# Local attention with a 7x7 dilated convolution, then whitening: a row of the first image by single taps, interpolations cut in two, and a new order of sums

## The chip, the cores and the metric

The kernel runs on one core of a Trainium2 chip. The time is device microseconds of one execution, launch to end. The profile is a trace of one execution by the hardware profiler. Engines: PE is TensorE (PEld its weight loads), DVE is VectorE, ACT is ScalarE, POOL is GpSimd, SP is SyncE, whose queue issues most DMAs.

## What is computed

All data are 32-bit floats; x is 4 images of 256 channels and 64 x 64 pixels.

```python
# layer 0: attention weights from a 7x7 convolution with dilation 2, then local sums
k = conv(x, w1, padding=6, dilation=2) + b1      # 256 -> 128 channels
k = conv1x1(k, w2) + b2                          # 128 -> 49 channels
attn = softmax(k, axis=channels)                 # one weight per tap of a 7x7 window
xp = pad(x, 6)
shifts = stack([xp[:, :, 2*u:2*u+64, 2*v:2*v+64] for u in range(7) for v in range(7)])
y = einsum('bkchw,bkhw->bchw', shifts, attn)
# layer 1: whitening of y in 4 groups of 64 channels
# Sigma = covariance of a group over all images and pixels; 5 Newton steps towards Sigma^(-1/2)
out = whiten(y) * weight + bias
```

## The kernel before, in words

Both convolutions are folded into one, 256 channels to 49 taps. With dilation 2 an image falls into four planes by the parity of row and column, and on each plane the 7x7 convolution is undilated. It is computed in Winograd form over rows and columns with the points 1, -1, 2, -2, 1/2, 0 and infinity (`EVAL`).

**A row point** (`rows`, `prepare`, `conv_step`). For one row point of one image VectorE combines rows of x into a buffer `rb` (`row_eval`), then for each column point combines columns into `xh` (`col_eval`). TensorE multiplies `xh` by transformed weights `wr` (`conv_bank`, line 466) in three banks of column points, (1, -1, 0), (2, -2, infinity) and (1/2), each into one of two PSUM buffers `cv`; ScalarE evicts each bank into `pv` (L475). VectorE then interpolates over columns (`col_interp`, 22 operations of 162 columns) into `zz`. `prepare` of the next row point follows each bank in the program, so `xh` and `wr` are filled as TensorE frees them. When all row points are done, `row_interp` does the same 22 operations of 576 columns over rows, and one ScalarE activation of 2048 columns adds the bias (L535). The result is the image's logits. The helpers `add`, `sub` and `madd` (lines 265, 268, 272) issue every VectorE operation of these steps, so one line of the profile stands for many.

**Weights** of a row point are formed by VectorE once, in the first image that uses them, scaled by ScalarE, stored to DRAM (`gd`, L384) and loaded again for later images (L330). Row point 1/2 (number 5) is not a Winograd row in image 0: its combined weights `gb5` are kept in DRAM (`g5d`) and its transformed weights are formed in image 1 from that copy.

**Image 0** takes row points 1, -1, 2 and -2 (numbers 1 to 4) in Winograd form. Points 0, 1/2 and infinity go by `direct` (L554): for each of the seven column taps and two channel halves, matmuls of up to 512 columns add into one half of the PSUM tile `acc`; a row point has two halves, `sr` 0 and 1 (infinity has one). ScalarE copies half 0 into `zz` (L565) or one row of half 1 (L567), and VectorE adds the rest. Order on TensorE: infinity, row 1, 0 (half 0), row 2, 0 (half 1), row 3, 1/2 (both halves), row 4; then infinity of image 1 (`direct_inf`) and its row 0. In images 1 to 3 only infinity is direct.

**Softmax and sums.** For each image and column parity `softmax` transposes the logits (L680), takes the maximum (L688, L691), exponentials with their sums (L696), and normalises (L710). `move_terms` copies the weights of one plane `n` (16 in all) into `zt` (16 copies, L738) and SyncE stores them to `sd`; `load_band` loads them skewed, in two parts, into `band`, and VectorE transposes them in place (L766). `zt` and `band` have one buffer each. TensorE then multiplies transposed blocks of x (`make_block`, L780, evicted by L787) by the band (`weighted_sum`, L808). The sums of a plane are two halves, `first_half` and `second_half`, evicted by L822 into the slot of x; `turn_y` transposes y (L837, evicted by L844) and `moments` (L857) adds up the covariance. Three PSUM buffers `tp` serve every transpose.

**The order of the work.** TensorE's order is the program's own (`pe`). The other engines' orders come from the scheduler of the build, and each engine runs its list in that order. A hand-written plan cuts the convolutions of an image into eight parts of equal cost and calls, in the gap after each, softmax steps and halves of sums of the image before (`plan`, `gap`). Softmax of an image stands in gaps 1 and 2 of the next one; the eight halves of images 0 and 1 in gaps 3, 4 (two of them), 5, 6, 7, 8, 9 of the next image, where 8 and 9 are gaps 0 and 1 of the one after. Image 2's halves begin in gap 3, image 3's after all convolutions. x of later images is loaded by GpSimd's queue after the finished slot is spilled to DRAM (`move`), and y is loaded back for the end (`back`), where out is written (L1116 to L1135).

Of the kernel before, what the change touches and what calls it, by code (L numbers as in the profile page):

```python
# [31 lines left out]
def kernel(  # L32
# [230 lines left out]

    def add(o, a, b):
        return TT(o, a, b, ALU.add)  # L265

    def sub(o, a, b):
        return TT(o, a, b, ALU.subtract)

    def madd(o, a, f, b):  # L270

        return STT(o, a, f, b, ALU.mult, ALU.add)  # L272
# [4 lines left out]
    g5d = dram.tile([P, KS * NSK], F32, name="g5d")  # L277

    def row_weights(br):
# [8 lines left out]
        if br == 1:  # L288
            add(E, T[6], T[4])
            add(O, T[5], T[3])  # L290
            add(S0, E, O)
            add(E1, T[2], T[0])
            add(S1, E1, T[1])
        elif br == 2:
            sub(S0, E, O)
            sub(S1, E1, T[1])
        elif br == 3:
            madd(E, T[4], 4.0, T[6])
            madd(O, T[3], 4.0, T[5])
            madd(S0, O, 2.0, E)  # L300
            madd(E1, T[0], 4.0, T[2])
            madd(S1, T[1], 2.0, E1)
        elif br == 4:
            madd(S0, O, -2.0, E)
            madd(S1, T[1], -2.0, E1)
        else:
            madd(S0, T[6], 2.0, T[5])
            madd(S0, S0, 2.0, T[4])
            madd(S0, S0, 2.0, T[3])
            madd(S1, T[2], 4.0, T[0])  # L310
            madd(S1, T[1], 2.0, S1)
            add(S1, S1, S1)
            f = gb5.rearrange("p v a r k -> p (v a r k)")
            nc.scalar.mul(f, f, SCALE[5])
            nc.sync.dma_start(g5d, f)

    def weights(b, br, i):
# [17 lines left out]
        elif br == 5:  # L335

            f = rb[0].rearrange("p q r c w -> p (q r c w)")[:, : KS * NSK]
            if i == 0:
                nc.sync.dma_start(f, g5d)
# [40 lines left out]
        for bc in BANKS[i]:  # L380
            f = SCALE[bc] * (SCALE[br] if br != 5 else 1.0)
# [98 lines left out]
    def interpolate(pt, tmp, outs, cut):  # L480
# [9 lines left out]
        add(tmp, s1, s2)  # L490
        sub(s2, s1, s2)
        add(s1, s3, s4)
        sub(s4, s3, s4)
        add(s3, c0, c6)
        madd(hh, tmp, 10.0 / 9, hh)
        madd(hh, s1, -1.0 / 9, hh)
        madd(hh, s3, 2.5, hh)
        sub(s3, tmp, s3)
        madd(s1, tmp, -2.0, s1)
        madd(s1, c0, 1.5, s1)  # L500
        madd(s1, c6, -30.0, s1)
        madd(s3, s1, -1.0 / 6, s3)
        sub(tmp, s4, s2)
        madd(hh, s2, 16.0 / 9, hh)
        madd(hh, tmp, -1.0 / 9, hh)
        madd(tmp, hh, -3.0, tmp)
        sub(s2, s2, hh)
        madd(s2, tmp, -1.0 / 15, s2)
        madd(outs[0], lo(s1), 1.0 / 6, hi(c0))
        madd(outs[1], lo(tmp), 1.0 / 15, hi(s2))  # L510
        add(outs[2], lo(c6), hi(s3))
        nc.scalar.copy(outs[3], lo(hh))
# [5 lines left out]
    def col_interp(br, pv):  # L518
        pt = {b: pv[:K2, i] for i, b in enumerate(ORDER)}
        outs = phases(zz[:K2, br].rearrange("p q (w two) -> p q w two", two=2))  # L520
        cut = lambda t, k: t[:, :, 2 * k : 2 * (k + Q8)].rearrange("p q (b two) -> p q b two", two=2)
        interpolate(pt, it[:K2], outs, cut)

    def row_interp(b):
# [8 lines left out]
        interpolate(pt, ct.rearrange("p a b -> p (a b)")[:K2, : Q9 * W].rearrange("p (q w) -> p q w", w=W), outs, lambda t, k: t[:, k : k + Q8])  # L533
        f = lg[:K2].rearrange("p r w -> p (r w)")
        nc.scalar.activation(f, f, AF.Identity, bias=bias[:K2])  # L535
        logits[b] = lg
# [47 lines left out]
    rows = [(0, br) for br in (1, 2, 3, 4)]  # L584
# [16 lines left out]
    def conv_step(k, i):  # L601
# [3 lines left out]
        if k + 1 < len(rows):  # L605
            prepare(k + 1, i)
        if i == len(BANKS) - 1:
            col_interp(br, pvs.pop((b, br)))
            if k + 1 == len(rows) or rows[k + 1][0] != b:
                row_interp(b)  # L610

    def direct0(br, sr):
        if br == 5:
            direct(0, br, sr, acc[:, sr], [gb5[:, v, :, sr] for v in range(KS)], x5)
# [6 lines left out]
    for k in range(NR0):  # L623
        if k == 2:
            row_weights(5)
            x5 = store[4].rearrange("p c r w -> p (c r w)")[:, SH * W :].rearrange(
                "p (q r c w) -> p q r c w", q=Q8, r=2, c=NCC
            )
            row_eval(0, 5, [rb[0], rb[1], x5])
# [4 lines left out]
        elif k == 2:  # L634
            direct0(5, 0)
            direct0(5, 1)

            for sr in range(2):
                nc.scalar.copy(
                    gr0[:, :, :, sr].rearrange("p v a k -> p (v a) k"),  # L640
                    tap[:, UPOS[KS - 1 - 4 * sr]].rearrange("p v a k -> p (v a) k"),
                )
        if k == 1:
            for s in range(2, 4):
                load_x(s, s, nc.gpsimd)
    gpool.release()
# [27 lines left out]
    def softmax(b, pc, hf):  # L674

        lv = logits[b].rearrange("p r w -> p (r w)")
        lt = tp().rearrange("p (i h k) -> p i h k", i=NI, h=2)
        for i in range(NI):
            pe(
                nc.tensor.transpose(  # L680
                    lt[:, i].rearrange("p h k -> p (h k)")[:, :K2],
                    lv[:K2, bass.ds(2 * (NI * hf + i) * P + pc, P, 2)],
                    ident[:K2, :K2],
                )
            )
        nm = f"{b}_{pc}_{hf}"
        mx = work.tile([P, NI, 2], F32, tag="mx", name=f"mx_{nm}")
        nc.vector.tensor_reduce(mx, lt[:, :, :, :KT], AX.X, ALU.max)  # L688
        if hf == 0:
            terms[b, pc] = bpool.tile([P, 2, NCH, KT], F32, tag="d", name=f"d_{b}_{pc}", bufs=2)  # L690
        nc.vector.tensor_scalar(mx, mx, -1.0, None, ALU.mult)  # L691
        d = terms[b, pc][:, :, NI * hf : NI * (hf + 1)]
        s = work.tile([P, 2, NI], F32, tag="s", name=f"s_{nm}")
        for h in range(2):
            for i in range(NI):
                nc.scalar.activation(  # L696
                    d[:, h, i], lt[:, i, h, :KT], AF.Exp,
                    bias=mx[:, i, h : h + 1], accum_out=s[:, h, i : i + 1],
                )
        nc.vector.reciprocal(s, s)  # L700
        rm = work.tile([P, 2, NI, KS], F32, tag="rm", name=f"rm_{nm}")
        nc.vector.tensor_tensor(
            rm.rearrange("p h i v -> p (h i) v"),
            s.rearrange("p h i -> p (h i)").unsqueeze(2).to_broadcast([P, NCH, KS]),
            cmask.unsqueeze(1).to_broadcast([P, NCH, KS]),
            ALU.mult,
        )
        for h in range(2):
            dh = d[:, h].rearrange("p i (u v) -> p i u v", u=KS)
            nc.vector.tensor_tensor(  # L710
                dh, dh, rm[:, h].unsqueeze(2).to_broadcast([P, NI, KS, KS]), ALU.mult
# [35 lines left out]
    BAND = ((0, 3), (3, 8))  # L747
# [26 lines left out]
    def make_block(n, m):  # L774
# [18 lines left out]
        ((6, 21, 31), (4, 16, 23), (3, 16, 19), (7, 25, 32), (5, 17, 27)),  # L793
# [129 lines left out]
    def bands(n):  # L923
# [4 lines left out]
        if n - 1 in done:  # L928
            load_band(n, 1)
            move_terms(n + 1)  # L930

    def second_half(n):
        turn_y(n, 0)
        turn_y(n, 1)
        weighted_sum(n, 1, 0)
        turn_y(n, 2)
        weighted_sum(n, 1, 1)
        turn_y(n, 3)
        make_block(n, 5)
# [19 lines left out]
    def soft(b, pc):  # L959
        for hf in range(2):  # L960
            softmax(b, pc, hf)
# [3 lines left out]
    for b in range(B):  # L965
# [5 lines left out]
        if b + 2 < B:  # L971

            plan(b + 1, 3, hs[0])
            plan(b + 1, 4, *hs[1:3])
            plan(b + 1, 5, hs[3])
            plan(b + 1, 5, finish)
            for j in range(4):
                plan(b + 1, 6 + j, hs[4 + j])
# [3 lines left out]
    for b in range(B):  # L982
        for j in range(2):
            plan(b + 1, j if b == B - 1 else j + 1, lambda b=b, j=j: soft(b, j))
# [124 lines left out]
    n = 0  # L1109
# [60 lines left out]
```

## Time and profile before

| | us |
|---|---|
| median of 3 runs | 819.41 (816.88 to 820.16) |
| the profiled execution | 819.8 |
| its span, first to last instruction | 818.0 |
| TensorE busy | 719.5 |
| VectorE busy | 598.4 |
| ScalarE busy | 365.3 |
| mean granted clock of TensorE | 0.947 |

A page's timeline shows one line per group of equal instructions: its start, its length, engine, line and operation, the tiles written and read, and in brackets the idle time of the engine ahead of it with what ended that idle time. A table of windows gives busy time of each engine in a stretch of the span. Matmuls are pipelined, so a busy TensorE isn't TensorE at its peak. VectorE's operations overlap a little at their ends: an operation on 576 columns lasts 0.75 us, and the next starts 0.67 us after it.

### The profile page before, as it was taken

The numbers are of one execution on the slowest core, as the hardware profiler recorded it, in microseconds if no ns is written. First come the engines' busy times: TensorE is split into PE (matmuls) and PEld (weight loads), VectorE is DVE, ScalarE is ACT, GpSimd is POOL, SyncE is SP. The second block draws the span as 40 slices with busy tenths as digits, with TensorE's granted clock in tenths as the row PEclk, the third lists the DMA queues.
The fourth block names the chain that finished last, engine by engine and source line by source line (L and its number), as shares of the span: only waits on it lengthen the run. The fifth ranks groups of instructions, "written<-read, shape, count | busy, mean of one in ns | idle before, by whom it ended". The sixth has DMA issues, their size and how long they took to land.

```text
span 818.0 us, 18531 instructions
## 1 busy us (share of the span) xinstructions
PE 719.5 (88%) x7540; PEld 555.6 (68%) x7540; DVE 598.4 (73%) x1300; ACT 365.3 (45%) x1067; POOL 35.1 (4%) x45
## 2 busy tenths in 40 slices
PE   5789997975768999999879999989999487998997
PEld 1356672655746996789759968888898366886443
DVE  2799999599779767989797579898966732214443
ACT  1323332214565344267553333686434575553443
POOL 0320000300000010000100100000000100000000
PEclk9979998997979999999989999998999698999999
DMA  8993001320744275045934931155411554310577
GB/s 332 197 285 111 32 36 65 107 82 20 199 153 133 105 230 149 19 165 149 250 103 130 262 104 31 48 162 183 139 53 46 212 211 123 109 46 1 232 305 286
DMA packets 57837, 114.66 MB, mean 140 GB/s; under 512 B 21607, under 2 KB 40856, under 8 KB 56472
## 3 DMA queue, kind: packets, MB, share of 16 engines
q1 hardware_dynamic: 53624, 88.31, 34.2%
q0 software_dynamic: 4128, 25.17, 10.5%
q8 instruction: 59, 0.97, 0.5%
q14 instruction: 26, 0.21, 0.1%
HBM read 66.83 MB, written 46.63 MB: 139 GB/s over the span
## 4 chain that ended last, share of the span: by engine, by line
PE 31%; DVE 24%; DMA 10%; ACT 9%; issue 4%; SPq 0%; POOL 0%; DVEq 0%; ACTq 0%; POOLq 0%
PE y L808 10%; PE tp L1116 7%; PE cv L466 6%; ACT zt L738 4%; DMA slot<-in_x_dram 4%; DVE zz L272 4%; DMA sd<-zt 3%; PE sig L857 3%; PE tp L780 3%; DVE xh L272 3%; DVE pv L272 3%; PE tp L837 2%; DMA spill<-slot 2%; DVE rb L272 2%; DVE band L766 1%
## 5 line engine op out<-in xcount | busy, mean ns | idle before, releaser
L466 PE MATMUL cv<-xh,wr 128*49 128x128 f32 (+1 forms) x4576 | 263.0, 276 | 3.7 <-DVE xh L265 3.5
L466 PEld LDWEIGHTS cv<-xh,wr 128*49 128x49 f32 x4576 | 256.1, 124 | 9.8 <-issue 5.3
L808 PE MATMUL y<-band,xb 128*128 128x320 f32 (+2 forms) x640 | 163.0, 391 | 21.7 <-ACT xb L787 15.1
L808 PEld LDWEIGHTS y<-band,xb 128*128 128x128 f32 x640 | 112.4, 205 | 38.1 <-ACT xb L787 18.2
L766 DVE STREAM_TRANSPOSE band<-band 128x960 f32<-128x960 f32 (+1 forms) x32 | 48.2, 1508 | 59.5 <-DMA band<-sd 42.8
L738 ACT COPY zt<-d 32x112 f32<-32x112 f32 x224 | 62.9, 281 | 37.6 <-DMA sd<-zt 19.0
L837 PE MATMUL tp<-ident,slot 128*128 128x128 f32 x256 | 52.8, 303 | 16.4 <-ACT yt L844 12.1
L837 PEld LDWEIGHTS tp<-ident,slot 128*128 128x128 f32 x256 | 43.1, 203 | 31.6 <-ACT yt L844 14.6
L822 ACT ACTIVATE slot<-y,pivot 128x512 f32<-128x512 f32 x64 | 43.1, 732 | 41.9 <-PE y L808 41.8
L475 ACT COPY pv<-cv 113x486 f32<-113x486 f32 (+1 forms) x66 | 31.7, 480 | 66.1 <-PE cv L466 66.0
L844 ACT COPY yt<-tp 128x256 f32<-128x256 f32 x128 | 44.9, 380 | 29.0 <-PE tp L837 27.3
L780 PE MATMUL tp<-ident,slot 128*128 128x128 f32 x256 | 51.7, 306 | 5.9 <-ACT yt L844 5.9
L787 ACT COPY xb<-tp 128x256 f32<-128x256 f32 x128 | 44.7, 375 | 20.8 <-PE tp L780 20.1
L780 PEld LDWEIGHTS tp<-ident,slot 128*128 128x128 f32 x256 | 40.7, 207 | 12.2 <-ACT yt L844 6.3
L1131 DVE TENSOR_SCALAR out<-tp,scale,beta 128x512 f32<-128x512 f32 x32 | 25.9, 810 | 29.5 <-PE tp L1116 29.5
L554 PE MATMUL acc<-slot,tap 128*49 128x480 f32 (+3 forms) x168 | 38.9, 608 | 4.6 <-DMA slot<-in_x_dram 4.6
L696 ACT ACTIVATE d<-tp,mx 128x49 f32<-128x49 f32 x128 | 36.5, 340 | 12.0 <-DVE mx L691 12.0
L857 PEld LDWEIGHTS sig<-yt 128*64 128x64 f32 x1024 | 33.5, 141 | 9.1 <-issue 7.6
L272 DVE SCALAR_TENSOR_TENSOR pv<-pv 113x162 f32<-113x162 f32 x132 | 39.1, 323 | 0.1
L1127 ACT ACTIVATE out<-tp,beta,scale 128x512 f32<-128x512 f32 x32 | 24.9, 778 | 31.7 <-PE tp L1116 31.7
L857 PE MATMUL sig<-yt 128*64 128x65 f32 x1024 | 38.0, 228 | 0.0
L272 DVE SCALAR_TENSOR_TENSOR xh<-ct 128x512 f32<-128x512 f32 x44 | 28.6, 686 | 12.5 <-PE cv L466 12.3
(196 smaller groups left out, 947.1 us busy)
## 6 DMA issues: line engine op xcount, KB each, us to landing
out_dram<-out SPq DMA_DIRECT2D x32, 512.0 KB, 2.6
sd<-zt SPq DMA_DIRECT2D x16, 896.0 KB, 4.5
slot<-in_x_dram POOLq DMA_DIRECT2D x12, 1024.0 KB, 13.1
wr<-gd SPq DMA_DIRECT2D x16, 588.0 KB, 4.8
band<-sd SPq DMA_DIRECT2D x64, 140.0 KB, 3.0
wr<-gd SPq DMA_DIRECT2D x16, 490.0 KB, 3.5
w<-in_L_conv_w_dram SPq DMA_DIRECT2D x4, 1568.0 KB, 11.3
spill<-slot POOLq DMA_DIRECT2D x3, 2048.0 KB, 7.7
```

The costliest lines, as they stand in the source:

```text
L272: return STT(o, a, f, b, ALU.mult, ALU.add)
L466: nc.tensor.matmul(cv[h * HB : h * HB + KT, k, sr : sr + n, sc : sc + n], wv[:, sc, sr, cc], xh[bc][:, :n, h * NCC + cc, :n], start=(j == ...
L738: nc.scalar.copy(o, i)
L766: nc.vector.transpose(f, f)
L780: nc.tensor.transpose(t[:, cc * P : (cc + 1) * P], xt[:, cc, CR * m : CR * (m + 1), bass.ds(pc, SW, 2)], ident,)
L787: nc.scalar.copy(xb, t[:, :C])
L808: nc.tensor.matmul(ps[:, cc, q0 - half * HALF : q1 - half * HALF, :], xb[:, cc * P : (cc + 1) * P], rhs, start=(k == 0), stop=(k == len(PI ...
L822: nc.scalar.activation(yt[:, cc, half * HALF : (half + 1) * HALF, bass.ds(pc, SW, 2)], ps[:, cc], AF.Identity, bias=pivot[:, cc : cc + 1],)
L837: nc.tensor.transpose(t[:, cc * P : (cc + 1) * P], yt[:, cc, CR * i : CR * (i + 1), bass.ds(pc, SW, 2)], ident,)
L844: nc.scalar.copy(yb.rearrange("p a g c -> p (a g) c")[:, :, :GW], t[:, :C].rearrange("p (e c) -> p e c", c=GW),)
L857: nc.tensor.matmul(sig[g * GW : (g + 1) * GW, cc], yb[:, cc, g, :GW], yb[:, cc, g], start=(count[0] == 0 and cc == 0), stop=(count[0] == 4 ...
L1116: nc.tensor.matmul(t, wm[cc], slots[2 * b + pr][:, cc, q * TR : (q + 1) * TR, :].rearrange("p r w -> p (r w)"), start=True, stop=True,)
```

## The change

1. **Image 0, row point -2 (number 4)** goes by single taps like 1/2: its Winograd row is gone, its combined weights `gbr` are kept in DRAM, and its transformed weights are formed in image 1. TensorE's order becomes infinity, row 1, 0 (half 0), row 2, 0 (half 1), row 3, then both halves of -2, both of 1/2, and infinity of image 1.
2. **Interpolations in two parts.** The formulas are rearranged, still 22 operations, so that 17 of them (part 0) need everything but point 1/2, and five (part 1) need it. At the end of image 0 the row interpolation's part 0 stands between the halves; in images 1 to 3 it stands after row 4, and part 1 after row 5. The bias is added by four activations of 512 columns, one for each row phase. The scratch of the row interpolation is the other image's `zi`, one row of which GpSimd clears again.
3. **VectorE's order** is written out for these steps alone (`in_order`): each operation of a block, and every later `add`, `sub` and `madd`, comes after the one before it.
4. **Softmax** takes both halves of rows in one go, one eighth earlier (gaps 0 and 1).
5. **Sums** of images 0 and 1 come one half per gap, from gap 2; the pieces of a second half are reordered so that blocks 4 and 3 come first.
6. **The band** is loaded in three parts, rows 0 to 3, 3 to 5 and 5 to 8; the middle part of the next plane is loaded inside the second half, as soon as blocks 4 and 3 are done.

The core of the diff:

```diff
+    def in_turn(ins):
+        if turn[0] is not None:
+            tc.add_manual_dep(
+                ins.ins,
+                turn[0],
+                mybir.DependencyInfo(mybir.DependencyClass.NoSync, mybir.DependencyReason.DATA),
+                reason="in_turn",
+            )
+        if strict[0]:
+            turn[0] = ins.ins.name
+        return ins
...
     def add(o, a, b):
-        return TT(o, a, b, ALU.add)
+        return in_turn(TT(o, a, b, ALU.add))
...
+        if part != 1:
+            add(tmp, s1, s2)
+            sub(s2, s1, s2)
+            add(s1, s3, s4)
+            sub(s4, s3, s4)
+            add(s3, c0, c6)
+            sub(s3, tmp, s3)
+            madd(s1, tmp, -2.0, s1)
+            madd(tmp, tmp, -30.5, s1)
+            madd(tmp, s3, 22.5, tmp)
+            madd(s1, c0, 1.5, s1)
+            madd(s1, c6, -30.0, s1)
+            madd(s3, s1, -1.0 / 6, s3)
+            sub(s4, s4, s2)
+            madd(tmp, s2, -16.0, tmp)
+            add(tmp, tmp, s4)
+            madd(outs[0], lo(s1), 1.0 / 6, hi(c0))
+            add(outs[2], lo(c6), hi(s3))
+        if part != 0:
+            madd(hh, tmp, -1.0 / 9, hh)
+            madd(s4, hh, -3.0, s4)
+            sub(s2, s2, hh)
+            madd(s2, s4, -1.0 / 15, s2)
+            madd(outs[1], lo(s4), 1.0 / 15, hi(s2))
...
-    rows = [(0, br) for br in (1, 2, 3, 4)]
+    rows = [(0, br) for br in (1, 2, 3)]
...
+        end = b > 0 and br == ROWS[-1]
+        if end:
+
+            with in_order():
+                if i == len(BANKS) - 2:
+                    col_interp(b, br, 0)
+                elif i == len(BANKS) - 1:
+                    col_interp(b, br, 1)
+                    row_interp(b, 1)
...
+            if b > 0 and br == ROWS[-2]:
+                with in_order():
+                    col_interp(b, br)
+                    row_interp(b, 0)
...
+    direct0(4, 0)
+    with in_order():
+        direct0(4, 1)
+        row_interp(0, 0)
+    direct0(5, 0)
+    for i in range(len(BANKS)):
+        prepare(NR0, i)
+    with in_order():
+        direct0(5, 1)
+        row_interp(0, 1)
...
-    BAND = ((0, 3), (3, 8))
+    BAND = ((0, 3), (3, 5), (5, 8))
...
-        ((6, 21, 31), (4, 16, 23), (3, 16, 19), (7, 25, 32), (5, 17, 27)),
+        ((4, 16, 23), (3, 16, 19), (5, 17, 27), (6, 21, 31), (7, 25, 32)),
...
         weighted_sum(n, 1, 0)
+        weighted_sum(n, 1, 1)
+        load_band(n + 1, 1)
         turn_y(n, 2)
-        weighted_sum(n, 1, 1)
+        make_block(n, 5)
         turn_y(n, 3)
-        make_block(n, 5)
...
-            plan(b + 1, 3, hs[0])
-            plan(b + 1, 4, *hs[1:3])
-            plan(b + 1, 5, hs[3])
-            plan(b + 1, 5, finish)
-            for j in range(4):
-                plan(b + 1, 6 + j, hs[4 + j])
+            for j in range(8):
+                plan(b + 1, 2 + j, hs[j])
+                if j == 3:
+
+                    plan(b + 1, 2 + j, finish)
...
-            plan(b + 1, j if b == B - 1 else j + 1, lambda b=b, j=j: soft(b, j))
+            plan(b + 1, j, lambda b=b, j=j: soft(b, j))
```

## What the change should do to the time, worked out before it ran

> **What bounds the kernel now.** I read the page's busy shares first, then the table of 20 us windows, then TensorE's own timeline with the idle time ahead of each group, and last what VectorE, ScalarE and SyncE did inside each idle stretch. TensorE is the bound on average:
>
> ```profile
> PE 719.5 (88%) x7540; PEld 555.6 (68%) x7540; DVE 598.4 (73%) x1300; ACT 365.3 (45%) x1067; POOL 35.1 (4%) x45
> ```
>
> but its 98.5 us of idle time lie in a few places. In the windows (columns: PE, PEld, DVE, ACT, POOL busy, granted clock, DMA share, GB/s) the reader is to see that where TensorE idles the granted clock falls, and that VectorE is full in the first two:
>
> ```profile
> 120.00:140.00 20.00, 14.83 (x60) 4.65 (x58) 20.00 (x56) 7.04 (x15) 0.00 (x0) 0.83 0.17 66
> 180.00:200.00 20.00, 7.26 (x96) 6.99 (x98) 19.76 (x36) 6.98 (x31) 0.00 (x0) 0.66 0.13 36
> 640.00:660.00 20.00, 11.57 (x79) 9.57 (x80) 10.26 (x28) 12.61 (x51) 2.13 (x6) 0.67 0.77 300
> ```
>
> TensorE's timeline names the waits (start, length, engine, line; in brackets the idle time before it and what ended it):
>
> ```profile
> 132.54 14.23 PE L554 MATMUL acc<-slot,gb 128*49 128x512 f32 x56 [5.17 <-ACT zz L565]
> 192.74 1.78 PE L680 MATMUL tp<-ident,slot 113*128 113x113 f32 x8 [13.19 <-ACT slot L535]
> 231.39 2.50 PE L808 MATMUL y<-band,xb 128*128 128x320 f32 x4 [10.90 <-ACT xb L787]
> 415.15 0.70 PE L837 MATMUL tp<-ident,slot 128*128 128x128 f32 x2 [6.08 <-ACT yt L844]
> 645.29 1.78 PE L680 MATMUL tp<-ident,lgx 113*128 113x113 f32 x8 [9.21 <-ACT lgx L535]
> 681.72 2.63 PE L808 MATMUL y<-band,xb 128*128 128x224 f32 x8 [3.87 <-DVE band L766]
> ```
>
> The 13.19 and 9.21 us are the row interpolations of images 0 and 3: the softmax transposes need the logits, which need 22 operations of 576 columns (starts 0.67 us apart, about 15 us), VectorE's last word in each image. VectorE is full in every window from 40 to 200 us but the one at 140, so image 0 is bound by VectorE and the rest by TensorE with local waits.
>
> **The change, part by part**, against the profiled execution: 819.8 us, span 818.0, 0.4 us above the median of the three runs.
>
> *A. Image 0.* VectorE loses row 4's column evaluation (two operations 1.13 us and seven 0.60 us from start to start: 6.5 us), its 22 column interpolations of 162 columns (0.237 apart: 5.2) and its 20 weight operations (0.273: 5.5), and gains one addition of 0.62: 16.6 us less. The 5.5 come back in image 1 (C). TensorE gets dearer: the Winograd row is 208 matmuls in 11.76 us (146.60 to 158.4); two halves of single taps are 2 x 56 matmuls, 11.55 us each undisturbed (68.83, 91.80). The new path from the end of row 3 (115.2): ScalarE now copies tap weights (1.44) and scales row 4's (1.35) ahead of an eviction of row 3, so its last bank waits 1.2; four halves 4 x 11.55 = 46.2; each half waits until the other half is evicted (the 5.17 above is that wait, then long because ScalarE stood behind a weight product; now 0.65 for a copy of 0.57, 1.0 for copy and addition, 1.05 behind the bias of finished phases), 2.7 in all; the point at infinity of image 1 11.55; transposes 1.2; two banks of image 1 9.98; transposes 1.2. Sum 74.0, so the third bank starts at 189.2. Before it started at 194.45: **-5.3 us**. VectorE covers this: its row-3 work ends about 126, its first seventeen row operations run from 141.0 to 152.4 beside the next half, image 1's first evaluation and weights (11.9) to 164.3, and the last five (3.4) plus ScalarE (0.65) end at 170.2; the transposes come at 176.8. If that 6.6 us cover went, every us beyond it would be a us.
>
> *B. First half of sums.* Softmax moves an eighth earlier, and so do the first sums. Before, 36.9 us went by between the first softmax's transposes (end 194.5) and the first sum (231.39), 23.6 of them with convolutions: ScalarE's second move of terms stood behind VectorE, which stood 6.11 us in a band transposition that waited for its DMA. In the new order VectorE normalises the second softmax ahead of the band. New chain from 177.9: VectorE's maximum, a 2.2 us row evaluation put ahead of the negation, exponentials 181.3 to 185.7, sixteen copies of terms (4.6) to 191.4, DMA about 5.5, second move of terms to 201.8 and only then the eviction of image 1's third bank. TensorE needs that accumulator: it waits about 1 + 5 us, and with the block copies the first sum starts at 209.5. The same place before, less one eighth of convolutions (11.8) not yet done, is 219.6. So A and B are -10.1, B **-4.8** (bounds: -10.9, the whole wait, and 0).
>
> *C. Rest of image 1.* Waits there sum to 6.9 us (1.4, 0.5, 0.7, 2.55, 1.71). One half per eighth spreads them, but VectorE gets the 5.5 us of row-4 weights, a 686 KB load and three stores on SyncE, and now has about 103 us of work until the softmax against 115 of TensorE's, with in-order waits between. I take waits of 9: **+2** (-5 to +9).
>
> *D. Images 2 and 3.* Waits of 17.0 us before (1.65, 2.96, 0.76, 0.16, 6.08; 1.67, 2.97, 0.72). The two near 1.66 follow a 2.00 us bias over all logits in front of an eviction; it is now four of 512 columns (the 512-column copy takes 0.62), spread. Image 3's 2.97 and 0.72 have an eighth more room. The 6.08 stays in kind: ScalarE holds a hoisted move of terms until the previous one has left,
>
> ```profile
> 412.64 1.19 ACT L738 COPY zt<-d 32x112 f32<-32x112 f32 x4 [10.70 <-DMA sd<-zt]
> ```
>
> and that DMA took 10.91 us against a median of 4.5 because a load of x ran beside it (393.5 to about 410). In the new order the same move stands ahead of a sum's store, with 7.1 us of convolutions as cover: 0.3 us of wait with the median DMA, 6.7 with the slow one. The Trainium skill's "DMA: Bandwidth & Descriptors", in "Issuing engines are not separate DMA queues", says that transfers from different issuing engines share the same sixteen DMA engines; so GpSimd's load would still slow SyncE's store, and by that rule the 6.7 applies rather than 0.3, and the whole sum would be 796. From the rows alone I take 5, nearer to the slow one, as the load still starts in the same half. With 7 for the rest, 12 against 17: **-5** (-12 to +5).
>
> *E. Tail.* After the last convolution VectorE has 5 column and 5 row operations left instead of 22 rows: 1.2 + 3.4, and ScalarE 0.65. The transposes are due at 636.1; the logits would be there at about 630. The 9.21 go, and the slow clock behind them (1.78 for transposes that take 1.12 at 659.94, 2.34 for sums that take 1.24, turns 0.63 for 0.39): 2.5. The band in three parts lets part two load inside the half that frees it, so the 3.87 and the slow stretch after it (about 2.5) go. Against it: the exponentials of both halves now hold two of the three transpose buffers together, and start one reduction later; before, the waits here were 5.6, now two of 4.1 (twelve exponentials of 0.275 and a reduction) with 1.5 of slow clock after each: 8.2 + 3.0 - 5.6 = +5.6. In all -9.2 - 2.5 - 3.9 - 2.5 + 5.6 = **-12.5** (-16 to -5). The Trainium skill's "TensorE: Matmul & The Clock Gate", "What's actually happening", has the clock fall to half after an idle window of about 3.4 us; by it each 4.1 us wait costs up to 1.7 more where the rows gave 1.5, and the sum would be 0.4 longer.
>
> The remaining parts I cost at nothing: SyncE issues 64 more band DMAs at 0.43 (27 us), spread over the whole span beside waits for TensorE that sum to 176 us in its queue; where such a queue stands in front of a move of terms it is in B and D. Splitting the interpolation keeps 22 operations; softmax loses one small operation per pixel column. VectorE's written order means that at each image's end it cannot slip the next evaluation past the last two evictions; image 2 and 3 leave it 30 us of sums and infinity as cover. Without that cover it is the slow rival.
>
> Sum: -5.3 - 4.8 + 2 - 5 - 12.5 = -25.6; 819.8 - 25.6 = **794 us**.
>
> **Rivals.**
> 1. *More goes than I count* (0.14): B's and D's waits vanish (-6 and -5 more): about 784. For: TensorE's work between halves is about 10 us everywhere. Against: ScalarE's moves of terms stay hoisted.
> 2. *VectorE becomes the bound in image 1* (0.22): with single taps TensorE no longer waits in image 0, and image 1 loses 10 us more to it: about 804, up to 814. For: 103 of 115 us. Against: 20 us of VectorE idle time between 240 and 320 before.
> 3. *It doesn't do what it says* (0.06): the logits come no earlier for the transposes since ScalarE's in-order bias waits; the 13.19 and 9.21 come back, with A's taps: about 817.
> 4. *Slower* (0.08): the written order starves TensorE. At the end of each of images 1 to 3 VectorE idles for the last two evictions (up to 10 us: one bank and a half of sums lie between), and the next row's evaluations come that much late. Price: three times the excess over the cover. It decides once the excess is above 8.5 us an image, as 3 x 8.5 eats the 25.6; at 11 it gives 819.8 - 25.6 + 33 = 827.
> My forecast (788 to 801) has 0.50.
>
> **Range and chances.** 783 to 811: below lie about 0.06, above about 0.14. Faster by over 0.5% (about what a measurement can tell from no change): 0.50 + 0.14 + 0.22 = 0.86; within 0.06; slower 0.08.
>
> **What would show it.** The profile after: three Winograd rows, then four halves of taps without a wait above 1.5 us, transposes without a wait near 177, third bank near 189; first sum near 209; a wait of some 5 us before it with ScalarE's eviction as releaser; one wait near 5 us in image 2 behind the terms' DMA; in the tail no wait for logits, two near 4 us for exponentials, none for the band. I am wrong if TensorE waits for VectorE's evaluations (xh or wr) by more than 10 us in image 1, or for the logits anywhere.

## The result, and the profile after

The change makes the kernel slower: 825.8 us, median of 4 runs (825.1 to 827.5), against 819.6 for the kernel before beside it. The ratio is 1.0085, 95% interval 1.0058 to 1.0112. The prediction was 794 us, 783 to 811, so its sign was wrong. The profiled execution has a span of 823.3 us (before 818.0). Engines of the changed kernel, from the page:

```profile
PE 733.2 (89%) x7444; PEld 554.1 (67%) x7444; DVE 596.5 (72%) x1262; ACT 365.1 (44%) x1070; POOL 35.8 (4%) x49
```

TensorE's work rose by 13.7 us (the taps cost 11.3 more than the Winograd row) and its idle time fell from 98.5 to 90.1 only. The same three windows as before (columns as there):

```profile
120.00:140.00 20.00, 18.36 (x92) 5.71 (x88) 7.59 (x26) 1.12 (x3) 0.00 (x0) 1.00 0.00 1
180.00:200.00 20.00, 15.54 (x262) 14.71 (x256) 17.94 (x49) 16.37 (x86) 1.68 (x1) 1.00 0.55 166
640.00:660.00 20.00, 6.40 (x20) 4.32 (x21) 6.46 (x19) 8.73 (x46) 0.00 (x0) 0.64 0.61 231
```

The reader is to see that VectorE is no longer full at 120 to 140, where image 0 was bound, and that the window at 640 got worse: 6.4 us of matmuls for 11.6 before, at a clock of 0.64. TensorE's timeline in the changed kernel:

```profile
139.19 11.59 PE L596 MATMUL acc<-slot,gb 128*49 128x512 f32 x56 [0.97 <-DVE zz L287]
152.89 11.59 PE L596 MATMUL acc<-slot,gb 128*49 128x512 f32 x56 [2.12 <-ACT zz L607]
175.78 1.21 PE L752 MATMUL tp<-ident,slot 113*128 113x113 f32 x8
191.57 5.53 PE L491 MATMUL cv<-xh,wr 128*49 128x128 f32 x96 [1.56 <-ACT pv L500]
...
204.54 6.77 PE L491 MATMUL cv<-xh,wr 128*49 128x128 f32 x80 [7.43 <-ACT pv L500]
212.81 1.34 PE L877 MATMUL y<-band,xb 128*128 128x320 f32 x4 [0.82 <-ACT xb L856]
...
536.98 11.44 PE L491 MATMUL cv<-xh,wr 128*49 128x128 f32 x176 [3.52 <-DVE pv L290]
...
638.31 1.12 PE L752 MATMUL tp<-ident,lgx 113*128 113x113 f32 x8
...
650.33 0.70 PE L906 MATMUL tp<-ident,slot 128*128 128x128 f32 x2 [8.61 <-ACT d L766]
...
658.08 0.70 PE L906 MATMUL tp<-ident,slot 128*128 128x128 f32 x2 [4.42 <-ACT yt L913]
```

Both waits for logits are gone (no time stands in brackets at 175.78 and 638.31), as is the wait for the band near 681. New are 7.43 ahead of the convolution bank before the first sums, 3.52 in image 3, and 8.61 and 4.42 in the tail. (Image 3's row names a VectorE operation, but the load of weights that SyncE issued at 531.08 and that took 5.8 us, shown in experiment 3, landed at 536.9.)

I cut every profile at points where both kernels have done the same work: the start of the point at infinity of images 2 and 3, the end of the last convolution, the first matmul of the whitening (its line is L1037 before, L1105 after). Lengths in us, for these two and for the runs of the next section:

| kernel | to image 2's infinity | image 2 | image 3 | tail, to whitening | whitening to end | ratio to before |
|---|---|---|---|---|---|---|
| before | 322.8 | 160.1 | 138.2 | 123.6 | 73.4 | 1 |
| after | 318.6 | 156.3 | 143.6 | 130.3 | 74.5 | 1.0085 |
| late_reload_after | 318.9 | 157.5 | 144.7 | 121.5 | 73.5 | 0.9959 |
| late_mix | 313.8 | 157.2 | 144.6 | 116.9 | 74.9 | 0.9854 |
| late_free | 319.6 | 154.9 | 141.1 | 118.9 | 73.4 | 0.9878 |
| late_wino | 319.4 | 160.9 | 143.8 | 121.6 | 73.1 | 1.0013 |
| best | 311.8 | 154.8 | 141.2 | 112.8 | 74.4 | 0.9732 |
| best_early | 315.8 | 157.1 | 142.1 | 122.8 | 73.4 | 0.9876 |
| best_band2 | 311.5 | 152.0 | 142.8 | 121.6 | 74.4 | 0.9808 |
| best_plan | 306.8 | 168.8 | 145.7 | 114.0 | 73.4 | 0.9888 |

From before to after: -4.2, -3.8, +5.5, +6.8, +1.1. The tail, for which I had -12.5, is where the forecast broke: it accounts for 19.3 of the 30.9 us between forecast and result.

Each row is one execution, so small differences need care. The pairs before and late_reload_before, after and late_reload_after, best and best_early give TensorE, VectorE and ScalarE the same instructions in the same order and differ only in when the reload in the tail starts and in the order of its three loads. Ahead of the tail they still differ by up to 4.0 us in a stretch (311.8 and 315.8 to image 2's infinity in best and best_early; 160.1 and 163.8 for image 2 in before and late_reload_before). A single difference of that size up to image 3 shows nothing by itself. The start of the tail repeats: from the last convolution to the first softmax transposes takes 19.75 us in both after and late_reload_after.

**What holds the tail.** The reload of the three spilled images (6.3 MB, GpSimd's queue) goes into space that the image phases give up; VectorE's last work on the logits releases it. GpSimd's timeline before:

```profile
643.27 0.20 POOL L1008 MEMSET blk<- 128x128 f32 x1 [181.99 <-DVE lgx L272]
643.81 0.56 POOL L1013 DMA_DIRECT2D back<-spill  x1 [0.34 <-POOL blk L1008]
```

and after:

```profile
630.80 0.29 POOL L1076 MEMSET blk<- 128x128 f32 x1 [2.83 <-DVE lgx L294]
631.34 0.56 POOL L1081 DMA_DIRECT2D back<-spill  x1 [0.24 <-POOL blk L1076]
```

Since the logits are done earlier, the reload begins 12.5 us earlier, and now it runs beside the loads of the next bands. What the DMAs of the tile `band` take from issue to landing between 600 and 700 us, before and then after:

```profile
DMA to landing us min/median/max: 1.9/2.3/4.9
```

```profile
DMA to landing us min/median/max: 1.7/2.1/15.3
```

The longest is 15.3 us instead of 4.9. (The Trainium skill's "DMA: Bandwidth & Descriptors", section "Issuing engines are not separate DMA queues", says that transfers started by different engines run interleaved on the same sixteen DMA engines. These rows agree: SyncE's band loads take up to 15.3 us while GpSimd's reload runs.) VectorE's timeline after shows who stands behind it:

```profile
630.87 1.17 DVE L835 STREAM_TRANSPOSE band<-band 128x960 f32<-128x960 f32 x1
644.76 0.84 DVE L835 STREAM_TRANSPOSE band<-band 128x640 f32<-128x640 f32 x1 [12.71 <-DMA band<-sd]
645.53 1.00 DVE L758 TENSOR_REDUCE mx<-tp 128x8 f32<-128x392 f32 x2
...
649.18 0.20 DVE L770 RECIPROCAL s<-s 128x8 f32<-128x8 f32 x1 [2.44 <-ACT d L766]
653.26 1.18 DVE L835 STREAM_TRANSPOSE band<-band 128x960 f32<-128x960 f32 x1 [3.88 <-DMA band<-sd]
654.37 0.18 DVE L772 TENSOR_TENSOR rm<-s,cmask 128x56 f32<-128x56 f32 x1
```

TensorE had the transposed logits ready near 639.4, but the maximum (L758) stands in VectorE's list behind a band transposition (L835) that waited 12.71 us for its DMA. The next band part (3.88 us) stands ahead of the normalisation (L772). ScalarE's exponentials wait for the first and its moves of terms for the second; its copy of `yt` is behind the moves, and TensorE waits for that: the 8.61 and the 4.42.

### The profile page after: what moved, and what is told of

Read it like the earlier page. It is cut to its first block, busy times and chain, and to the rows that moved or that the text cites. A ratio compares the mean times of both kernels' runs of the same rounds, so it can differ in the third digit from the quotient of the medians.

```text
span 823.3 us, 18421 instructions
## 1 busy us (share of the span) xinstructions
PE 733.2 (89%) x7444; PEld 554.1 (67%) x7444; DVE 596.5 (72%) x1262; ACT 365.1 (44%) x1070; POOL 35.8 (4%) x49
## 4 chain that ended last, share of the span: by engine, by line
PE 56%; DVE 17%; ACT 14%; DMA 9%; issue 3%; SPq 0%; DVEq 0%; ACTq 0%
PE y L877 14%; PE cv L491 13%; ACT zt L807 7%; PE acc L596 7%; PE tp L1184 7%; DMA sd<-zt 4%; PE sig L926 3%; PE tp L849 3%; PE cv L596 3%; PE tp L906 3%; DMA band<-sd 2%; ACT d L766 2%; DVE xh L294 2%; PE cv L210 2%; DVE rb L287 2%
## 5 line engine op out<-in xcount | busy, mean ns | idle before, releaser
L491 PE MATMUL cv<-xh,wr 128*49 128x128 f32 x4368 | 254.1, 278 | 21.0 <-ACT pv L500 9.4
L491 PEld LDWEIGHTS cv<-xh,wr 128*49 128x49 f32 x4368 | 247.2, 125 | 26.4 <-ACT pv L500 10.2
L877 PE MATMUL y<-band,xb 128*128 128x224 f32 (+2 forms) x640 | 163.3, 397 | 9.9 <-ACT xb L856 9.8
L877 PEld LDWEIGHTS y<-band,xb 128*128 128x128 f32 x640 | 117.7, 206 | 34.9 <-ACT xb L856 14.3
L835 DVE STREAM_TRANSPOSE band<-band 128x960 f32<-128x960 f32 (+1 forms) x48 | 51.0, 1061 | 62.2 <-DMA band<-sd 42.2
L906 PEld LDWEIGHTS tp<-ident,slot 128*128 128x128 f32 x256 | 41.3, 206 | 34.6 <-ACT d L766 11.2
L849 PE MATMUL tp<-ident,slot 128*128 128x128 f32 x256 | 51.8, 306 | 12.4 <-ACT yt L913 11.3
L500 ACT COPY pv<-cv 113x486 f32<-113x486 f32 (+1 forms) x63 | 30.1, 479 | 59.6 <-PE cv L491 59.3
L856 ACT COPY xb<-tp 128x256 f32<-128x256 f32 x128 | 45.0, 375 | 23.2 <-PE tp L849 22.1
L849 PEld LDWEIGHTS tp<-ident,slot 128*128 128x128 f32 x256 | 40.6, 207 | 20.3 <-ACT yt L913 13.0
L596 PE MATMUL acc<-slot,tap 128*49 128x480 f32 (+3 forms) x168 | 35.8, 570 | 1.7 <-DMA slot<-in_x_dram 1.7
L408 ACT ACTIVATE wr<-wr 128x392 f32<-128x392 f32 (+1 forms) x36 | 17.1, 510 | 43.8 <-DVE wr L287 27.5
```

What stands on the lines that cost most here:

```text
L491: nc.tensor.matmul(cv[h * HB : h * HB + KT, k, sr : sr + n, sc : sc + n], wv[:, sc, sr, cc], xh[bc][:, :n, h * NCC + cc, :n], start=(j == ...
L596: nc.tensor.matmul(ps[h * HB : h * HB + KT, :, w0:w1_], w[v][:, cc], xs[:, :, cc, w0 + d : w1_ + d], start=(j == 0), stop=(j == len(order) ...
L835: nc.vector.transpose(f, f)
L849: nc.tensor.transpose(t[:, cc * P : (cc + 1) * P], xt[:, cc, CR * m : CR * (m + 1), bass.ds(pc, SW, 2)], ident,)
L856: nc.scalar.copy(xb, t[:, :C])
L877: nc.tensor.matmul(ps[:, cc, q0 - half * HALF : q1 - half * HALF, :], xb[:, cc * P : (cc + 1) * P], rhs, start=(k == 0), stop=(k == len(PI ...
```

## The experiments

Ratios are to the kernel before beside each run; 0.01 is 8.2 us, and a difference of two ratios is uncertain by some 3 to 5 us (two half intervals of 0.0022 to 0.0053, added as squares). Added lines shift the line numbers; operations and tiles keep their names.

**1. The reload later.** Each of the three loads gets a dependency on a store of sums of image 3, so they start at 683, 691 and 699 us. They come in the order 2, 1, 0; nothing else in the program changes (diff shortened):

```diff
-    for k in range(3):
+    def reload(k, after):
...
-        nc.gpsimd.dma_start(t.rearrange("p a r w -> p (a r w)"), spill[k])
+        dma = nc.gpsimd.dma_start(t.rearrange("p a r w -> p (a r w)"), spill[k])
+        tc.add_manual_dep(dma.ins, mark[after].ins.name, <Sync, DATA>, reason="reload")
...
+    late = {(4, 3): (2, (12, 0)), (4, 4): (1, (12, 1)), (4, 5): (0, (13, 0))}
     for k in sorted(todo):
         gap(*k)
+        if k in late:
+            reload(*late[k])
```

> The changed kernel, but the three reloads of spilled images (6.3 MB) start only after image 3's first three halves of sums are stored, instead of as soon as the logits have left. Theory 'collision': in the changed kernel the reload starts at 631 us instead of 643.8, the band loads beside it take up to 15.3 us instead of about 2, and VectorE's band transposition, which waits for them, stands ahead of the softmax's maximum (TensorE waits 8.61 us) and again ahead of its normalisation (4.42). Then the stretch from the last convolution to the whitening falls from 130.3 us by 10 to 14 (8.61 to about 3.5, 4.42 to under 1, 2 to 4 of slow clock), and the time to 812 to 816. Rival 'buffers': the exponentials of both halves hold two of three transpose buffers; then nothing changes, 823 to 827.

Measured: 817.1 us, ratio 0.9959 (0.9937 to 0.9981), by the ratios 10.3 us less than the changed kernel. The tail fell by 8.8 us. VectorE in this run:

```profile
637.20 0.84 DVE L835 STREAM_TRANSPOSE band<-band 128x640 f32<-128x640 f32 x1 [2.61 <-DMA band<-sd]
641.52 1.06 DVE L758 TENSOR_REDUCE mx<-tp 128x8 f32<-128x392 f32 x2 [3.48 <-PE tp L752]
```

and TensorE:

```profile
646.38 0.50 PE L908 MATMUL tp<-ident,slot 128*128 128x128 f32 x2 [2.11 <-ACT d L766]
...
650.35 0.70 PE L908 MATMUL tp<-ident,slot 128*128 128x128 f32 x2 [1.26 <-ACT yt L915]
```

The band's transposition is over before TensorE's transposes of the logits; 8.61 became 2.11 and 4.42 became 1.26. Only the reload differs between the two kernels, so the collision is shown. The time is 1 us above the expected 812 to 816, and the drop in the tail a little short of the 10 to 14 expected, as the halves after 691 us take 1.5 us longer beside the reload, 1.12 of it a wait for the band.

The same reload in the **kernel before**:

> The kernel before with the same late reload. Theory 'collision': there the reload starts at 643.8, when the bands for the next sums have landed, and meets the softmax and the move of terms (10.5 us median to landing); only the stalls behind that go (0.61, 2.42 and part of 3.87 us with slow clock), so 813 to 818. If the reload costs nothing beside the sums there: 819 to 820.

Measured: 829.3 us, 1.0095 (1.0063 to 1.0127): slower, a miss for both readings. The reload now meets the steady sums, whose band comes in two parts:

```profile
707.29 2.63 PE L808 MATMUL y<-band,xb 128*128 128x224 f32 x8 [7.89 <-DVE band L766]
...
726.81 1.41 PE L808 MATMUL y<-band,xb 128*128 128x224 f32 x8 [1.93 <-DVE band L766]
```

At 643.8 it had lain beside the softmax, where it cost less: the tail takes 133.4 us here for 123.6. In late_reload_after the longest such wait is 1.12 us, with the band in three parts; experiment 4 takes this up.

**2. The joint softmax.** First the changed kernel with the softmax of each half by itself again (`for hf in range(2): softmax(b, pc, hf)`, the old body):

> The changed kernel with the softmax of the kernel before (each half by itself: maximum, exponentials, normalisation). Theory 'collision': the first half's maximum still stands behind the band transposition until 645.5 us; only the eight exponentials of the second half (2.2 us) come off the 8.61 us wait, so 822 to 826. Rival 'buffers': the waits of 8.61 and 1.91 and the slow clock behind them go, 815 to 819.

Measured: 825.9 us, 1.0052 (1.0019 to 1.0085). In the tail the wait is still 7.62 us, 1 us less, as 'collision' has it. But the stretches moved both ways: to image 2's infinity 312.1 (-6.5), image 2 164.2 (+7.9), image 3 147.4 (+3.8), tail 128.1 (-2.2). So halves help where image 0 ends, perhaps a little where image 3 does, and hurt in image 2, where the softmax of image 1 lies between convolutions (image 3's +3.8 is no more than single executions differ by); what makes that loss was not taken apart. Hence the mixture, on top of the late reload (diff shortened):

```diff
+    HALVED = (0, 3)
     def soft(b, pc):
-        softmax(b, pc)
+        if b in HALVED: softmax_h(b, pc, 0); softmax_h(b, pc, 1)   # as before the change
+        else: softmax(b, pc)
```

> The changed kernel with the late reload (817.1 us in its run), and the softmax in separate halves again for images 0 and 3 alone. Theory 'sixteen exponentials': the joint softmax costs where it stands alone on the path: in image 1 the stretch from its point at infinity to the first sum fell from 48.5 to 41.2 us with halves, and in the tail the exponentials held two transpose buffers (waits of 2.11, 1.26, 1.91, 2.36 with slow clock). Then 806 to 811. Rival 'only shifted': with halves everywhere images 2 and 3 lost 7.9 and 3.8 us, as they came 6.5 us earlier to the same transfers; then image 2 gives the gain back and the time is 813 to 818.

Measured: 808.4 us, 0.9854 (0.9811 to 0.9898), 8.6 us less than with the late reload alone; image 2 keeps its 157. The rival falls. ScalarE shows the reason near the first sum. Changed kernel:

```profile
199.54 4.62 ACT L807 COPY zt<-d 32x112 f32<-32x112 f32 x16 [2.78 <-DMA sd<-zt]
204.19 0.76 ACT L500 COPY pv<-cv 113x162 f32<-113x162 f32 x2
```

late_mix:

```profile
197.82 0.40 ACT L500 COPY pv<-cv 113x162 f32<-113x162 f32 x1
199.30 4.63 ACT L847 COPY zt<-d 32x112 f32<-32x112 f32 x16 [1.09 <-DMA sd<-zt]
```

With the joint softmax two evictions (L500, x2) stand behind the second move of terms and its DMA wait; with halves the scheduler puts one of them, which TensorE needs, ahead. The 7.43 us are gone; 3.00 remain ahead of the first sum:

```profile
206.64 2.50 PE L917 MATMUL y<-band,xb 128*128 128x320 f32 x4 [3.00 <-ACT xb L896]
```

4.7 us of the tail go too, where one transpose buffer comes free after eight exponentials.

**3. VectorE's written order, and image 0.** On top of the late reload `in_order` is made to do nothing (`strict[0] = False`); the interpolations stay split:

> The changed kernel with the late reload, without VectorE's written order at the ends of images; the interpolations stay split. If the written order is what has the logits ready for the transposes, TensorE waits for logits again in the tail (9.21 us before the change) and in image 1: 821 to 828. If the split alone does it, and the order only makes ScalarE stand behind VectorE's parts (the half before the softmax takes 12.2 us against 7.4 before): 812 to 816.

Measured: 809.7 us, 0.9878 (0.9826 to 0.9931), 6.6 us less than late_reload_after and below both ranges, without a wait for logits. The split alone has them ready. Images 2 and 3 and the tail are each some 3 us shorter. Image 0 is 7.1 longer (its infinity for image 1 starts at 172.8 for 165.7, with a wait of 7.99 for a tap half), but image 1 makes up 6.4 of that by image 2's infinity. In the tail ScalarE's list shows what the order cost. late_reload_after:

```profile
628.11 0.33 ACT L555 COPY zz<-pv 113x144 f32<-113x144 f32 x1 [1.79 <-DVE pv L294]
628.33 1.31 ACT L893 ACTIVATE slot<-y,pivot 128x512 f32<-128x512 f32 x2
630.29 0.72 ACT L578 ACTIVATE lgx<-zz,bias 113x512 f32<-113x512 f32 x1 [0.64 <-DVE zz L294]
630.91 0.62 ACT L856 COPY xb<-tp 128x256 f32<-128x256 f32 x2
```

ScalarE waits 1.79 and 0.64 us for VectorE's interpolation parts with the store of sums (L893) and the block copies (L856) behind it; TensorE stands 1.24 and 0.85 us for those:

```profile
631.32 0.70 PE L908 MATMUL tp<-ident,slot 128*128 128x128 f32 x2 [1.24 <-ACT xb L856]
631.82 2.50 PE L877 MATMUL y<-band,xb 128*128 128x224 f32 x8
...
636.08 3.18 PE L877 MATMUL y<-band,xb 128*128 128x320 f32 x12 [0.85 <-ACT xb L856]
```

Its granted clock is 0.50 from 631.3 to 634.1, and the eight sums there take 2.50 us where eight of the same shape took 1.36 at 625.69. Two halves of sums take 19.8 us there (621.0 to 640.9) and 16.6 in late_free (615.4 to 632.0).

Next, on the late reload, image 0 with row point -2 as a Winograd row again (`rows` 1 to 4, its loop as before, which also takes VectorE's written order out of image 0):

> The changed kernel with the late reload, with row point -2 of image 0 as a Winograd row again, in the kernel before's order of work in image 0. By my step A the taps are worth 5.3 us, as image 0 waits for VectorE otherwise: 820 to 824, with a wait for the logits ahead of image 1's transposes. Rival: TensorE's 11.3 us of extra taps eat what they save, and it is the same within 2 us: 815 to 819.

Measured: 821.1 us, 1.0013 (0.9987 to 1.0038), 4.4 more than late_reload_after. The wait is back, longer than the 13.19 before, as the softmax now comes one eighth of convolutions (11.8 us) earlier:

```profile
190.38 1.78 PE L745 MATMUL tp<-ident,slot 113*128 113x113 f32 x8 [22.15 <-ACT slot L578]
```

But its first sum stands at 222.7 for 214.7, 8.0 us later, and image 2's infinity only 0.5 later. In late_reload_after the rest of image 1 has two waits for ScalarE's copies that late_wino lacks (2.77 at 236.86, 2.91 at 299.90): most of what image 0 gains is given back there. Another 3.4 us come in image 2, no more than single executions differ by there.

**Moves of terms.** Two more suspects, one kernel each. The first is the changed kernel with the terms' DMA issued by ScalarE (`nc.scalar.dma_start(sd[...])`), since SyncE shows in image 3

```profile
530.65 0.34 SPq L811 DMA_DIRECT2D sd<-zt  x1
531.08 2.74 SPq L355 DMA_DIRECT2D wr<-gd  x3
```

that the weights' loads, 5.8 us to landing, come behind the terms' DMA just ahead of the 3.52 us wait:

> The changed kernel with the terms' DMA issued by ScalarE instead of SyncE. Theory 'queue': in image 3 the convolution at 536.98 us waited 3.52 us for weights whose load was issued at 531.08, right behind the terms' DMA at 530.65, which waited in SyncE's queue for ScalarE's copies; the load needs 5.8 us. Then that wait and 1.5 us of slow clock go, image 3 (143.6 us from its point at infinity to its last convolution) falls to about 138.5, and the time to 819 to 822. Rival 'VectorE': VectorE's band transpositions and normalisations make the evaluation late; then nothing changes, 824 to 827.

Measured: 834.6 us, 1.0163 (1.0112 to 1.0214), 6.4 more. The 3.52 went (0.76 stood there), but image 3 grew to 146.7 us: 20 us later TensorE waited for ScalarE:

```profile
559.15 0.70 PE L849 MATMUL tp<-ident,slot 128*128 128x128 f32 x2 [7.15 <-ACT yt L913]
```

The theory names the wait and not what the stretch costs, and the time lies above both ranges. The second, on the late reload, keeps each copy of terms behind the last store of sums in the program text (diff shortened):

```diff
+        held = mark[max(mark)] if mark else None
-                    nc.scalar.copy(o, i)
+                    ins = nc.scalar.copy(o, i)
+                    if held is not None:
+                        tc.add_manual_dep(ins.ins, held.ins.name, <NoSync, DATA>, reason="hold")
```

> The changed kernel with the late reload, and ScalarE's copies of terms kept behind the store of sums that the program text puts ahead of them, so that the scheduler can't hoist them in front of the convolutions' evictions. Theory 'hoisted terms': in images 1 to 3 ScalarE stands in these copies (waiting for the terms' DMA) ahead of evictions that TensorE needs, and SyncE stands in the terms' DMA ahead of a weights' load (3.78 us and slow clock in image 3); then images 2 and 3 lose 5 to 8 us together and the time is 809 to 813. Rival 'late bands': the bands come that much later, VectorE's transposition or TensorE's sums wait for them, and the time is 817 to 825.

Measured: 826.6 us, 1.0070 (1.0043 to 1.0096), 9.1 more than late_reload_after. Image 2 took 163.3, the tail 127.8. TensorE waits 5.52 us (image 1), 4.47 (image 2) and 2.27 (tail) for block copies (L866) that now stand behind the moves (L810), as ScalarE shows in image 2:

```profile
438.72 4.61 ACT L810 COPY zt<-d 32x112 f32<-32x112 f32 x16
443.36 0.65 ACT L866 COPY xb<-tp 128x256 f32<-128x256 f32 x2
```

Hoisting the moves is worth more than it costs; my theory fell, and the rival's late bands are not what TensorE waits longest for.

**4. Put together, and taken out again.** `best` has the late reload, halves for images 0 and 3, and the written order in image 0 alone; the other three each undo one thing in it.

> The changed kernel with the late reload, halves of the softmax in images 0 and 3, and VectorE's written order in image 0 alone. Theory 'three causes that add up': against the late reload (817.1) the halves gave 8.7 us (image 0 and tail) and taking the order away gave 2.7 in image 2, 3.6 in image 3, 2.7 in the tail, 1.1 in image 1, and cost 7 in image 0, where it is kept: 797 to 803. Rival 'the same wait twice': the halves and the free order both only shorten the waits for ScalarE; then 804 to 808.

Measured: 797.9 us, 0.9732 (0.9699 to 0.9765): faster than both kernels, 22.0 us under the kernel before. The causes add, within what the ratios can tell.

> The run 'best' with the reload as the changed kernel has it, as soon as the logits have left. Theory 'collision': VectorE's band transposition waits for a slow DMA ahead of the maximum, whatever the softmax and the order: 6 to 10 us more than 'best'. Rival: the collision needed the joint softmax or the written order: within 2 us of 'best'.

Measured: 809.6 us, 0.9876 (0.9841 to 0.9912), 11.8 more than best; 10.0 of it lies in the tail of the profiled execution. The collision needs neither the joint softmax nor the order. VectorE, and then TensorE:

```profile
641.99 0.84 DVE L873 STREAM_TRANSPOSE band<-band 128x640 f32<-128x640 f32 x1 [17.42 <-DMA band<-sd]
642.76 1.00 DVE L795 TENSOR_REDUCE mx<-tp 128x8 f32<-128x392 f32 x2
...
646.29 0.70 PE L944 MATMUL tp<-ident,slot 128*128 128x128 f32 x2 [11.46 <-ACT d L803]
```

> The run 'best' with the band in two parts and the pieces and second halves in the order of the kernel before. Theory 'parts give slack': with two parts the late reload made the kernel before 9 us slower (waits of 7.89 and 1.93 us for band transpositions in the steady sums), so 5 to 10 us more than 'best'. Rival: that loss had to do with the kernel before's order: within 2 us of 'best'.

Measured: 804.1 us, 0.9808 (0.9775 to 0.9841), 6.2 more; the tail is 8.8 longer (121.6 for 112.8), with waits of 3.24 and, in the steady sums,

```profile
680.87 2.64 PE L915 MATMUL y<-band,xb 128*128 128x224 f32 x8 [7.54 <-DVE band L873]
```

That is late_reload_before's loss again: it goes with the two parts and the order of pieces that belongs to them. The two were changed together, so which of them decides is not shown.

> The run 'best' with softmax and sums in the eighths of the kernel before (softmax one eighth later in images 1 to 3, sums one, two and one in three eighths). By my step B the earlier place is worth 4.8 us in image 1 and by D up to 5 in images 2 and 3: 3 to 8 us more than 'best'. Rival: the place is worth nothing where TensorE has convolutions to do anyway: within 2 us.

Measured: 811.0 us, 0.9888 (0.9857 to 0.9919), 12.8 more, above the 3 to 8 expected. It splits: 5.0 less up to image 2's infinity, 14.0 more in image 2 and 4.4 in image 3.

## Why the prediction was wrong, by its own steps

**A, image 0 (-5.3): right in kind, half the size.** The third bank started at 191.57 for a predicted 189.2 and 194.45 before: -2.9. The halves of taps waited 0.68, 0.97 and 2.12 us, where I had nothing over 1.5, and the bank 1.56. Undoing the step, and the written order in image 0 with it, cost 4.4 us in all, but hardly any of it by the end of image 1.

**B, first sums (-4.8): mechanism right, A and B together -6.8 for -10.1.** The eviction behind the second move of terms came as foreseen, but TensorE waited 1.56 + 7.43 + 0.82 us for my 6; the first sum stood at 212.8 for 209.5. I took the wait as the price of the early place. Most of it was the price of the joint softmax: late_mix has 0.70 and 3.00 in its place. And the earlier place itself gains nothing up to the end of image 1 (best_plan is 5.0 better there); it pays in image 2 (14.0).

**C, rest of image 1 (+2): right, as far as single executions can tell.** From 6.8 us ahead at the first sum (212.8 against the same place before at 219.6) to 4.2 at image 2's infinity: +2.6.

**D, images 2 and 3 (-5): wrong in image 3.** Image 2 gave -3.8, without the 5 us wait that I took from a terms' DMA beside a load of x. The load began at 375.6 us for 393.5 before; the terms' DMA of 382.14 ran beside it and took 8.1 us, but TensorE's longest wait in the image is 1.79: the slow transfer came, and the wait that I hung on it did not. Image 3 gave +5.5 for an expected gain. Without the written order, which I had costed at nothing, it is 3.6 shorter (late_free), but single executions differ by as much. The 3.52 us wait for weights behind the terms' DMA is of the kind that I named for SyncE's queue only in B and D's move of terms; moving that DMA took the wait away and did not shorten the image. Even best is 3.0 us slower here than before, with 6.13 us of wait for ScalarE; so the cause in image 3 stays open.

**E, tail (-12.5): the step that failed; measured +6.8.** Its removals came true: no wait for logits (-9.2), none for the band (-5.5 with the slow clock behind it, for -6.4). The two softmax stretches (from the transposes of the first softmax to those of the second, and on to the next half of sums) were to change by -2.5 for slow clock and +5.6 for the exponentials, +3.1; without the collision, in late_reload_after, they take 16.57 and 17.16 us against 14.65 and 12.94 before, +6.1. So this price was 3 us short. What failed is the step's silence on what the earlier logits set off: it put nothing for the reload that they release. The first softmax stretch took 26.8 us in the changed kernel and 16.6 with the late reload: 10.2 us of collision. The passage on what "I cost at nothing" hides another 4.8: the two halves ahead of the softmax take 19.8 us for 15.0 before, and 3.2 of that goes without the written order; where the other 1.6 comes from was not traced. So the tail is -9.2 (logits) - 5.5 (band and the slow clock behind it) + 6.1 (softmax stretches) + 10.2 (collision) + 4.8 (ahead of the softmax) + 0.3 (the rest) = +6.7, with rounding.

In sum: -4.16 - 3.80 + 5.45 + 6.75 + 1.06 = +5.30 between the spans, against -25.6. best, with the late reload, the halves and the written order in image 0 alone, is at -22.0 by its ratio. The collision alone decides the sign and not the whole miss: with the late reload the time is still 817.1, above my range, and the joint softmax (8.6 us in late_mix) and the written order (6.6 in late_free) are most of what remains.

**The rivals.** 1 and 3 did not come. 2 has a trace in image 1, which gives back most of image 0's gain, but TensorE waits there for ScalarE and the size is 2.6 us. Rival 4 has the sign and, at 827, nearly the time, but not the cause: the written order cost 6.6 us in all on the late reload (some 3 us an image, at the edge of what single executions show), where it was to decide above 8.5 an image, and between the first sum and the tail every wait of TensorE in the changed kernel but the 3.52 is for ScalarE, none for VectorE's evaluations. The cause that decided, the collision, was no rival of mine: I asked what cover the logits' wait would leave, and not which transfer was waiting for the logits too.

## What to carry to other kernels

When a change makes a result ready earlier, list everything that its completion releases, memory and the transfers that wait for that memory too, and look at what runs in that window: here 12 us of earlier logits started a 6.3 MB reload in front of the band loads, and the 10.3 us that this cost turned a gain of 0.4% into a loss of 0.85%. A transfer that nobody needs soon wants a start of its own. And before a step is called free because the engine has idle time, read what stands behind it in the in-order lists of the engines that consume its result: a written order on VectorE was paid by ScalarE's list.

## What the runs showed that was not expected

One band DMA took up to 15.3 us beside the reload, seven times the median of 2.1 us. With its transposition cut into parts of 640 and 960 columns instead of one of 1600, and the pieces reordered to match, the same late reload cost little in steady sums (longest wait 1.12 us against 7.89 in the kernel before). And keeping ScalarE's copies of terms behind the sums' stores, against the scheduler's choice, cost 9.1 us.
